# Two adder convolutions, rebuilt from four channels over half an image to one channel over a whole image

## The chip, the cores and the metric

The kernel runs on one core of one Trainium2 chip. The metric is the time of one execution on the device in microseconds (us), the median of three runs. The engines are TensorE (PE in the profile; its weight loads are PEld), VectorE (DVE), ScalarE (ACT), GpSimd (POOL) and SyncE (SP, which here only issues transfers). They run side by side, each works through its own instructions in order, and they meet through semaphores.

## The reference, cut to what matters

A batch of 4 images of 128 channels by 64 by 64 positions goes through four layers: attention over positions, a pair of shift and adder convolutions, a gated attention block, and a selective scan. The change is in the second layer, which does this twice, the second time on the normalised result of the first:

```python
def shift_conv(x, w):            # 3x3 convolution, weights rounded to powers of two
    return conv(x, shift_quant(w), padding=1)

def adder_conv(x, w):            # 3x3, stride 1, pad 1: out = -sum |patch - weight|
    patches = conv_general_dilated_patches(x, (3, 3), padding=1)
    p = patches.reshape(N, Cin * 9, H * W)
    def per_channel(wc):
        return -jnp.sum(jnp.abs(p - wc[None, :, None]), axis=1)
    return lax.map(per_channel, w.reshape(Cout, Cin * 9))

out = relu(batchnorm(adder_conv(shift_conv(x, w_shift1), w_add1)))
out = batchnorm(adder_conv(shift_conv(out, w_shift2), w_add2))
return relu(out + x)
```

For each of 128 output channels, each of 9 taps and each image, 128 input channels by 4096 positions of absolute differences are formed and summed over the input channels. No matrix product gives that, and these two sums take two thirds of the kernel.

## The kernel before, in words

All data are fp32, with the 128 channels on the partitions. `shift_adder` (from L266) is called twice; its tiles carry the prefix a1 in the first call and a2 in the second. It quantises the shift weights (L276, L277 and the function above it), convolves image 0 (L319), and then loops over the images. While image b goes through the adder part, the convolution of image b+1 is drawn from a generator, a matmul at a time, between the adder's own matmuls.

**One term, three ways.** |p - w| is formed by ScalarE as an activation (Abs with the weight as a bias, L392), or, since |p - w| = 2 max(p, w) - p - w, by VectorE as a maximum (L403). The nine taps of a channel are shared out: taps 4, 5, 6 and half of tap 7 (scaled by one half) go to ScalarE, taps 0 to 3 to VectorE, and tap 8 is added by VectorE into the tile that ScalarE made for tap 7 (maximum and add in one instruction, L421, in place). A channel so makes 8 tiles: 4 of ScalarE and 4 of VectorE. The sums of p and of w that the maxima leave over are added apart: w as `wsum`, p by matmuls against ones (L348).

**The sum over channels.** TensorE sums a tile over its 128 partitions by a matmul with a weight of 32 columns, of which one is -1 or -2 and the rest 0 (`gather`, L338). The column lands the sum in one row of 32; four column groups of the array take four matmuls at once. In the kernel before, the four groups stand for four output channels, 32 apart.

**The order.** Work goes by image, by half an image (2048 positions), by jj from 0 to 31, and by q from 0 to 3. One q is what I call a step: four channels (32 g + jj), one ScalarE tile and one VectorE tile of 128 by 2048 for each, one L421, 16 gathers of the VectorE tiles and 16 of the ScalarE tiles. Four steps finish four channels for half an image. A half has 128 steps, and a call of `shift_adder` has 1024. The pools give VectorE's tiles 7 buffers and ScalarE's 8 (L293, L294), each of half an image; the sums of a half sit in four PSUM banks, taken from six. In each half, 20 full-width matmuls put the sum of p into the banks (L348), four with the first step and one with each of the next 16. At the end of a half the banks are evicted (L363), counted into the statistics (L364) and stored (L365).

A scheduler orders each engine's instructions ahead of time from the order in which the program states them, and gives out the buffers of each pool; what an engine waits for is then fixed. `layer1` (L437) makes the batch norm's scale from the statistics and gives the second call a loader that normalises the whole image as it comes in (L460 to L462).

Of the kernel before, what the change touches and what calls it, by code (L numbers as in the profile page):

```python
# [8 lines left out]
F32 = mybir.dt.float32  # L9
# [8 lines left out]
B = 4  # L18
# [7 lines left out]
TAPS = 9  # L26

# [12 lines left out]
def rows(ap):  # L40

    return ap.rearrange("p (r w) -> p r w", w=W)
# [223 lines left out]
def shift_adder(tc, cm, load, w_shift, w_add, stats, y_d, tag):  # L266
# [3 lines left out]
    nc = tc.nc  # L270
    with ExitStack() as ctx:
        cp = ctx.enter_context(tc.tile_pool(name=f"{tag}c", bufs=1))
        wqs = cp.tile([P, TAPS, P], F32, name=f"{tag}wq")
        with tc.tile_pool(name=f"{tag}q", bufs=1) as qp:
            ws = qp.tile([P, TAPS * P], F32, name=f"{tag}ws")
            nc.sync.dma_start(ws, w_shift)  # L276
            quantize(nc, qp, ws, wqs.rearrange("p t o -> p (t o)"), tag)  # L277
# [13 lines left out]
        xin_pool = ctx.enter_context(tc.tile_pool(name=f"{tag}x", bufs=1))  # L291
        pb_pool = ctx.enter_context(tc.tile_pool(name=f"{tag}p", bufs=2))
        dp = ctx.enter_context(tc.tile_pool(name=f"{tag}d", bufs=7))  # L293
        ap = ctx.enter_context(tc.tile_pool(name=f"{tag}a", bufs=8))  # L294
        ep = ctx.enter_context(tc.tile_pool(name=f"{tag}e", bufs=2))
        ps_c = ctx.enter_context(tc.tile_pool(name=f"{tag}pc", bufs=2, space=PSUM))
        ps_a = ctx.enter_context(tc.tile_pool(name=f"{tag}pa", bufs=6, space=PSUM))
# [3 lines left out]
        pw = ps_c.tile([P, 1], F32, tag="cv", name=f"{tag}pw")  # L301
        for i, t in enumerate(sum_taps):
            nc.tensor.matmul(pw, wa[:, t, :], cm.one_col, start=(i == 0), stop=(i == len(sum_taps) - 1))
        wsum = cp.tile([P, 1], F32, name=f"{tag}wsum")
        nc.vector.tensor_copy(wsum, pw)

        def fetch(b):
            t = xin_pool.tile([P, HP, HP], F32, tag="xin", name=f"{tag}xin{b}")
            clear_border(nc, t)
            load(b, t[:, 1 : 1 + H, 1 : 1 + W])  # L310
            return t

        def convolution(b, xin, pb):

            for k in range(NB):
                pc = ps_c.tile([P, BK], F32, tag="cv", name=f"{tag}pc{b}_{k}")
                for t in range(TAPS):
                    y, x = divmod(t, 3)
                    nc.tensor.matmul(  # L319
                        pc,  # L320
                        wqs[:, t, :],
                        xin[:, RB * k + y : RB * (k + 1) + y, x : x + W],
                        start=(t == 0),
                        stop=(t == TAPS - 1),
                    )
                    if t == TAPS - 1:
                        nc.vector.tensor_copy(pb[:, 1 + RB * k : 1 + RB * (k + 1), 1 : 1 + W], rows(pc))
                    yield
# [6 lines left out]
        def gather(pa, s, jj, group):  # L335

            for g, (v, d) in enumerate(group):
                nc.tensor.matmul(  # L338
                    pa[s][32 * g : 32 * g + 32, :],
                    pick[v][:, 31 - jj : 63 - jj],  # L340
                    d[:, bass.ts(s, BK)],
                    start=False, stop=False, skip_group_check=True,
                )

        def sum_of_p(pa, s, pb, half, t):
            y, x = divmod(t, 3)
            r = half * H // 2 + RB * s + y
            nc.tensor.matmul(  # L348
                pa[s], cm.ones, pb[:, r : r + RB, x : x + W],
                start=(t == sum_taps[0]), stop=False, skip_group_check=True,  # L350
            )

        def sums_of_p(pa, pb, half):
            for t in sum_taps[1:]:
                for s in range(4):
                    sum_of_p(pa, s, pb, half, t)
                    yield

        def evacuate(b, half, pa):
            for s in range(4):  # L360
                k = 4 * half + s
                o = ep.tile([P, BK], F32, tag="ev", name=f"{tag}ev{b}_{k}")
                nc.vector.tensor_scalar(o, pa[s], wsum, None, ALU.add)  # L363
                nc.vector.bn_stats(stats[:, NB * b + k, :], o)  # L364
                nc.sync.dma_start(y_d[b, :, bass.ts(k, BK)], o)  # L365

        pb = padded(0)
        for _ in convolution(0, fetch(0), pb):
            pass
        done = None  # L370
        for b in range(B):
            pb_next, steps = None, None
            for half in range(2):

                def view(t):
                    y, x = divmod(t, 3)
                    r0 = half * H // 2 + y
                    return pb[:, r0 : r0 + H // 2, x : x + W]

                pa = None  # L380
                for jj in range(32):
                    if b < B - 1 and half == 0 and jj == 1:
                        pb_next = padded(b + 1)
                        steps = convolution(b + 1, fetch(b + 1), pb_next)
                    for q in range(4):

                        act = [None] * 4
                        for g in [q] + [g for g in range(4) if g != q]:
                            co = 32 * g + jj
                            t = HALF_TAP if g == q else ACT_TAPS[q if q < g else q - 1]  # L390
                            at = ap.tile([P, HL], F32, tag="ab", name=f"{tag}a{b}_{half}_{co}_{t}")
                            nc.scalar.activation(  # L392
                                rows(at), view(t), AF.Abs, bias=wn[t][:, co : co + 1],
                                scale=0.5 if g == q else 1.0,
                            )
                            act[g] = (-2.0 if g == q else -1.0, at)

                        dve = []
                        t = DVE_TAPS[q]
                        for g in range(4):  # L400
                            co = 32 * g + jj
                            dt = dp.tile([P, HL], F32, tag="ad", name=f"{tag}d{b}_{half}_{co}_{t}")
                            nc.vector.tensor_scalar(  # L403
                                rows(dt), view(t), wa[:, t, co : co + 1], None, ALU.max
                            )
                            dve.append((-2.0, dt))
                        if pa is None:
                            if done:
                                evacuate(*done)
                            pa = []  # L410
                            for s in range(4):
                                pa.append(ps_a.tile([P, BK], F32, tag="pa", name=f"{tag}pa{b}_{half}_{s}"))
                                sum_of_p(pa, s, pb, half, sum_taps[0])
                                gather(pa, s, jj, dve)
                            sums = sums_of_p(pa, pb, half)
                        else:
                            for s in range(4):
                                gather(pa, s, jj, dve)
                        co = 32 * q + jj
                        at = rows(act[q][1])  # L420
                        nc.vector.scalar_tensor_tensor(  # L421
                            at, view(MAX_TAP), wa[:, MAX_TAP, co : co + 1], at, ALU.max, ALU.add
                        )
                        for s in range(4):
                            gather(pa, s, jj, act)
                        next(sums, None)
                        if steps and (q == 1 or q == 3 and jj % 4 < 2):
                            next(steps, None)
                done = (b, half, pa)
            if steps:  # L430
                for _ in steps:
                    pass
            pb = pb_next
# [3 lines left out]
def layer1(tc, cm, w_shift1, w_add1, g1, b1, w_shift2, w_add2, g2, b2, x1d, y1d, y2d):  # L437


    nc = tc.nc  # L440

    def batchnorm_scale(stats, gamma, name):
        mv = cm.pool.tile([P, 2], F32, name=f"mv{name}")
        nc.vector.bn_aggr(mv, stats.rearrange("p a s -> p (a s)"))
        sc = cm.pool.tile([P, 1], F32, name=f"sc{name}")
        cm.rstd(nc, sc, mv[:, 1:2])
        nc.vector.tensor_tensor(sc, sc, gamma, ALU.mult)
        return mv[:, 0:1], sc

    vec = {}  # L450
    for name, src in (("g1", g1), ("b1", b1), ("g2", g2), ("b2", b2)):
        vec[name] = cm.pool.tile([P, 1], F32, name=f"bn_{name}")
        nc.sync.dma_start(vec[name], col(src))

    stats1 = cm.pool.tile([P, B * NB, 6], F32, name="stats1")
    shift_adder(tc, cm, lambda b, t: nc.sync.dma_start(t, rows(x1d[b])), w_shift1, w_add1, stats1, y1d, "a1")
# [747 lines left out]
```

## Time and profile before

| what | us |
|---|---|
| median of three runs | 23555.58 (23554.83 to 23556.7) |
| the profiled execution, its own time | 23557.55 |
| its span from first to last instruction | 23555.8 |
| first call's adder part, from ScalarE's first Abs to its last | 2049.9 to 9944.4 |
| second call's adder part | 10030.0 to 17926.5 |

The page gives busy times of an execution: PE 21606.2 us (92% of the span), DVE 20116.0 (85%), ACT 19647.4 (83%), POOL 3766.7 (16%). Those are averages over stages with different limits. In the groups of instructions, each row is a line, engine and operation, with shapes, count, busy time, mean length of one in ns, and the idle time before it. The strip of forty digits cuts the span into slices, each digit a tenth of busy time. In the timeline, each row is a start, a length, and a run of equal instructions with no idle time between them, so that the spacing of n equal instructions is the length less that of one, over n - 1. A matmul of fp32 appears as two records.

### The profile page before, as it was taken

What the parts mean: (1) busy time and instruction counts of PE and PEld (TensorE: products, weight loads), DVE (VectorE), ACT (ScalarE), POOL (GpSimd) and SP (SyncE); (2) the same over time, 40 slices, a digit from 0 to 9 for tenths busy, and PEclk for the clock granted to TensorE, in tenths of its full rate; (3) what the DMA queues carried; (4) which work ended last, traced back from release to release, by engine and by line L of the source; (5) the groups of instructions that cost most, each with busy time, mean ns of one, the idle gap of its engine ahead of it and who ended that gap; (6) DMA issues with size and microseconds to landing.
All of it is one profiled execution on the core that took longest, in us unless ns stands there. A gap on an engine that the chain in (4) does not pass through costs nothing. (4 is left out here: it accounts for less than half of the span.)

```text
span 23555.8 us, 348033 instructions
## 1 busy us (share of the span) xinstructions
PE 21606.2 (92%) x146624; PEld 7799.2 (33%) x146624; DVE 20116.0 (85%) x15018; ACT 19647.4 (83%) x13700; POOL 3766.7 (16%) x1710
## 2 busy tenths in 40 slices
PE   9999999999999999999999999999997567677777
PEld 4443333333333333333333333333332222222222
DVE  7887999999999999889999999999997665777776
ACT  5666999999999999899999999999996336555555
POOL 5662000000000000000000000000000000577776
PEclk9999999999999999999999999999998776899999
DMA  0000000000000000000000000000000002788876
GB/s 14 9 5 12 1 3 7 1 3 5 3 3 1 3 1 3 8 5 3 5 3 1 5 5 1 3 1 3 3 1 32 0 3 96 182 195 194 194 192 163
DMA packets 174504, 809.07 MB, mean 34 GB/s; under 512 B 22716, under 2 KB 23364, under 8 KB 102788
## 3 DMA queue, kind: packets, MB, share of 16 engines
q1 hardware_dynamic: 172356, 778.42, 13.0%
q8 instruction: 1146, 18.78, 0.3%
q10 hardware_dynamic: 576, 8.39, 0.1%
q14 instruction: 426, 3.49, 0.0%
HBM read 658.15 MB, written 128.58 MB: 33 GB/s over the span
## 5 line engine op out<-in xcount | busy, mean ns | idle before, releaser
L392 ACT ACTIVATE a1a<-a1pb,a1wn 128x2048 f32<-128x2048 f32 x4096 | 7793.2, 2001 | 198.3 <-PE a1pa L338 101.3
L392 ACT ACTIVATE a2a<-a2pb,a2wn 128x2048 f32<-128x2048 f32 x4096 | 7791.9, 1999 | 136.2 <-PE a2pa L338 94.0
L403 DVE TENSOR_SCALAR a2d<-a2pb,a2wa 128x2048 f32<-128x2048 f32 x4096 | 4993.4, 1281 | 212.9 <-PE a2pa L338 212.4
L403 DVE TENSOR_SCALAR a1d<-a1pb,a1wa 128x2048 f32<-128x2048 f32 x4096 | 4992.1, 1281 | 207.2 <-PE a1pa L338 206.9
L338 PE MATMUL a2pa<-a2a,a2pick 128*32 128x512 f32 x32768 | 4576.3, 593 | 31.5 <-ACT a2a L392 31.5
L338 PE MATMUL a1pa<-a1a,a1pick 128*32 128x512 f32 x32768 | 4569.2, 593 | 31.5 <-ACT a1a L392 31.5
L338 PE MATMUL a2pa<-a2d,a2pick 128*32 128x512 f32 x32768 | 4436.8, 594 | 46.3 <-DVE a2d L403 46.0
L338 PE MATMUL a1pa<-a1d,a1pick 128*32 128x512 f32 x32768 | 4434.3, 594 | 47.2 <-DVE a1d L403 46.9
L421 DVE SCALAR_TENSOR_TENSOR a1a<-a1pb,a1wa,a1a 128x2048 f32<-128x2048 f32 x1024 | 2406.1, 2350 | 323.6 <-ACT a1a L392 323.6
L421 DVE SCALAR_TENSOR_TENSOR a2a<-a2pb,a2wa,a2a 128x2048 f32<-128x2048 f32 x1024 | 2406.1, 2350 | 314.1 <-ACT a2a L392 314.1
L338 PEld LDWEIGHTS a2pa<-a2a,a2pick 128*32 128x32 f32 x32768 | 1489.1, 110 | 2370.1 <-issue 2061.7
L338 PEld LDWEIGHTS a1pa<-a1a,a1pick 128*32 128x32 f32 x32768 | 1486.9, 110 | 2370.7 <-issue 2045.3
L962 PE MATMUL mg<-h,ident 128*128 128x512 f32 x4096 | 1982.8, 634 | 298.1 <-ACT m L971 227.4
L338 PEld LDWEIGHTS a2pa<-a2d,a2pick 128*32 128x32 f32 x32768 | 1347.1, 109 | 2472.1 <-issue 1935.5
L338 PEld LDWEIGHTS a1pa<-a1d,a1pick 128*32 128x32 f32 x32768 | 1345.4, 109 | 2471.8 <-issue 1913.8
L947 DVE TENSOR_TENSOR_SCAN h<-da,h,dbu 128x1024 f32<-128x1024 f32 x768 | 1804.2, 2349 | 87.0 <-POOL dbu L933 4.7
L962 PEld LDWEIGHTS mg<-h,ident 128*128 128x128 f32 x4096 | 787.1, 201 | 1529.4 <-issue 856.9
L186 POOL TENSOR_TENSOR ssum<-ssum,et 128x512 f32<-128x512 f32 x960 | 1230.3, 1282 | 232.9 <-ACT et L181 166.1
L975 POOL TENSOR_TENSOR m<-m,C 128x2048 f32<-128x2048 f32 x256 | 1157.7, 4522 | 605.2 <-ACT m L971 435.9
L933 POOL TENSOR_TENSOR dbu<-du,B 128x2048 f32<-128x2048 f32 x256 | 1153.6, 4529 | 26.3 <-DMA du<-du_d 26.3
L151 ACT COPY et<-pe 128x512 f32<-128x512 f32 x1024 | 596.6, 583 | 591.6 <-PE pe L149 575.9
L149 PE MATMUL pe<-q,k 128*128 128x512 f32 x2048 | 1051.1, 596 | 8.6 <-DVE mx L159 8.1
(267 smaller groups left out, 13672.1 us busy)
## 6 DMA issues: line engine op xcount, KB each, us to landing
dl<-delta_d SPq DMA_DIRECT2D x256, 1024.0 KB
du<-du_d SPq DMA_DIRECT2D x256, 1024.0 KB
xs_d<-xs SPq DMA_DIRECT2D x8, 2048.0 KB
sz_d<-sz SPq DMA_DIRECT2D x64, 256.0 KB
delta_d<-dv SPq DMA_DIRECT2D x32, 512.0 KB
du_d<-du SPq DMA_DIRECT2D x32, 512.0 KB
y_d<-ye SPq DMA_DIRECT2D x64, 256.0 KB
yx<-xs_d SPq DMA_DIRECT2D x64, 256.0 KB
```

Of the source, the lines that this page charges most:

```text
L149: nc.tensor.matmul(pe, k[:, bass.ts(j, P)], unit[u, "q"], start=True, stop=True)
L151: nc.scalar.copy(et, pe)
L186: nc.gpsimd.tensor_tensor(unit[u, "sum"], unit[u, "sum"], at, ALU.add)
L338: nc.tensor.matmul(pa[s][32 * g : 32 * g + 32, :], pick[v][:, 31 - jj : 63 - jj], d[:, bass.ts(s, BK)], start=False, stop=False, skip_grou ...
L392: nc.scalar.activation(rows(at), view(t), AF.Abs, bias=wn[t][:, co : co + 1], scale=0.5 if g == q else 1.0,)
L403: nc.vector.tensor_scalar(rows(dt), view(t), wa[:, t, co : co + 1], None, ALU.max)
L421: nc.vector.scalar_tensor_tensor(at, view(MAX_TAP), wa[:, MAX_TAP, co : co + 1], at, ALU.max, ALU.add)
L933: nc.gpsimd.tensor_tensor(t, du, by_states(b, h)[0], ALU.mult)
L947: nc.vector.tensor_tensor_scan(t[:, cols][:, s], da[:, s], st[n, "dbu", h][:, cols][:, s], 0.0 if e % 4 == 0 else st["last"], ALU.mult, AL ...
L962: nc.tensor.matmul(pm, cm.ident, st[n, way, h][:, bass.ts(k, BK)], start=(way == 0), stop=(way == 1))
L975: nc.gpsimd.tensor_tensor(m, m, by_states(tiles[n][0], h)[1], ALU.mult)
```

## The change

`shift_adder` is rebuilt around a whole image and one channel at a time:

- A tile is 128 by 4096, a whole image. The four column groups of TensorE take four position blocks of 512 of one channel's tile, and two PSUM banks take the eight blocks. A row of the banks is a channel, and 32 channels fill them.
- Every fourth channel (`extra`) adds tap 3 by a maximum and add in place into the tile of tap 1, so that it has two of those and 7 tiles to gather, and not 8.
- The sums of p are made once an image, in column groups, copied to a tile, and added at the eviction. They are drawn from the same generator as the next image's convolution.
- VectorE's tiles have 3 buffers and ScalarE's 4, of a whole image each.
- The convolution's input comes in 8 blocks of rows (with one row beside on either end) from 3 buffers, and not as an image; the normalising of the second call goes by block too.
- Both quantisations stand ahead of the first call.
- Rows of the statistics no longer stand where the channels do, so they go to DRAM and back ahead of the scale.

```diff
-        dp = ctx.enter_context(tc.tile_pool(name=f"{tag}d", bufs=7))
-        ap = ctx.enter_context(tc.tile_pool(name=f"{tag}a", bufs=8))
+        dp = ctx.enter_context(tc.tile_pool(name=f"{tag}d", bufs=3))
+        ap = ctx.enter_context(tc.tile_pool(name=f"{tag}a", bufs=4))
...
-        xin_pool = ctx.enter_context(tc.tile_pool(name=f"{tag}x", bufs=1))
+        xin_pool = ctx.enter_context(tc.tile_pool(name=f"{tag}x", bufs=3))
...
+        def gather(pa, jj, v, d, first=False):
+
+            for k in range(2):
+                for g in range(4):
+                    nc.tensor.matmul(
+                        pa[k][32 * g : 32 * g + 32, :],
+                        pick[v][:, 31 - jj : 63 - jj],
+                        d[:, bass.ts(4 * k + g, BK)],
+                        start=first, stop=False, skip_group_check=True,
+                    )
...
+        def evacuate(b, c, pa, sp):
+            for k in range(2):
+                o = ep.tile([P, BK], F32, tag="ev", name=f"{tag}ev{b}_{c}_{k}")
+                nc.vector.scalar_tensor_tensor(o, pa[k], wsum[:, c : c + 1], sp[:, k, :], ALU.add, ALU.add)
+                nc.vector.bn_stats(stats[:, c, 2 * b + k, :], o)
+                to = y_d[b, 32 * c : 32 * c + 32, :].rearrange("j (k g w) -> k g j w", k=2, g=4)
+                nc.sync.dma_start(to[k], o)
...
+                ah = absolute(HALF_TAP)
+                d = maximum(DVE_TAPS[0])
+                if late:
+                    gather(*late)
+                gather(pa, jj, -2.0, d, first=(jj == 0))
...
+                d = maximum(DVE_TAPS[1])
+                if extra:
+                    plus_maximum(d, DVE_TAPS[3])
+                else:
+                    gather(pa, jj, -2.0, d)
+                a = absolute(ACT_TAPS[0])
+                if co % 3 < 2:
+                    next(steps, None)
+                gather(pa, jj, -1.0, a)
+                a = absolute(ACT_TAPS[1])
+                if extra:
+                    gather(pa, jj, -2.0, d)
+                    gather(pa, jj, -1.0, a)
+                    plus_maximum(ah, MAX_TAP)
+                    gather(pa, jj, -2.0, ah)
+                    d = maximum(DVE_TAPS[2])
+                    a = absolute(ACT_TAPS[2])
+                    gather(pa, jj, -1.0, a)
+                    late = (pa, jj, -2.0, d)
+                else:
+                    plus_maximum(ah, MAX_TAP)
+                    gather(pa, jj, -2.0, ah)
+                    gather(pa, jj, -1.0, a)
+                    d = maximum(DVE_TAPS[2])
+                    gather(pa, jj, -2.0, d)
+                    a = absolute(ACT_TAPS[2])
+                    d = maximum(DVE_TAPS[3])
+                    gather(pa, jj, -2.0, d)
+                    late = (pa, jj, -1.0, a)
...
+        nc.sync.dma_start(at, stats.rearrange("p c s v -> p c (s v)"))
+        byco = lp.tile([P, 4, 2 * B * 6], F32, name=f"byco{name}")
+        for c in range(4):
+            nc.sync.dma_start(
+                byco[32 * c : 32 * c + 32], at[:, c, :].rearrange("(g j) s -> j g s", g=4)
             )
```

`absolute`, `maximum` and `plus_maximum` are the three instructions of L392, L403 and L421 with tiles of 4096. Names below: h is the tile of tap 7 (with tap 8 added in), a4 to a6 are ScalarE's other tiles, d0 to d3 VectorE's.

## The prediction

> **What bounds the kernel now.** First the strip of the page, to see where the engines are full:
>
> ```profile
> PE   9999999999999999999999999999997567677777
> DVE  7887999999999999889999999999997665777776
> ACT  5666999999999999899999999999996336555555
> PEclk9999999999999999999999999999998776899999
> ```
>
> From digit 5 to 30 three engines stand at nine tenths together. That stage is the two adder parts; the windows (PE, PEld, DVE, ACT and POOL busy) give it exactly:
>
> ```profile
> 2049.90:9944.40 7894.50, 7815.85 (x66276) 2741.18 (x66278) 7351.58 (x5197) 7793.11 (x4096) 5.33 (x10) 1.00 0.01 3
> 10030.00:17926.50 7896.50, 7818.72 (x66276) 2744.18 (x66278) 7357.29 (x5200) 7802.38 (x4099) 5.26 (x10) 1.00 0.01 3
> ```
>
> Which engine binds is seen in the timeline. A stretch without sums of p:
>
> ```profile
> 10499.75 32.35 ACT L392 ACTIVATE a2a<-a2pb,a2wn 128x2048 f32<-128x2048 f32 x17
> ...
> 10501.77 2.35 DVE L421 SCALAR_TENSOR_TENSOR a2a<-a2pb,a2wa,a2a 128x2048 f32<-128x2048 f32 x1 [0.46 <-ACT a2a L392]
> 10504.04 4.87 DVE L403 TENSOR_SCALAR a2d<-a2pb,a2wa 128x2048 f32<-128x2048 f32 x4
> 10509.37 2.35 DVE L421 SCALAR_TENSOR_TENSOR a2a<-a2pb,a2wa,a2a 128x2048 f32<-128x2048 f32 x1 [0.47 <-ACT a2a L392]
> ```
>
> ScalarE never pauses; VectorE waits for it each step. Its spacing is (32.35-2.00)/16 = 1.897 us, a step is 4 x 1.897 = 7.59. A stretch with sums of p:
>
> ```profile
> 8001.02 1.13 PE L348 MATMUL a1pa<-a1pb,ones 128*128 128x512 f32 x2
> 8002.08 3.64 PE L338 MATMUL a1pa<-a1d,a1pick 128*32 128x512 f32 x32
> 8005.54 3.62 PE L338 MATMUL a1pa<-a1a,a1pick 128*32 128x512 f32 x32
> ...
> 8001.17 7.70 ACT L392 ACTIVATE a1a<-a1pb,a1wn 128x2048 f32<-128x2048 f32 x4 [0.41 <-PE a1pa L338]
> 8009.23 7.70 ACT L392 ACTIVATE a1a<-a1pb,a1wn 128x2048 f32<-128x2048 f32 x4 [0.36 <-PE a1pa L338]
> ```
>
> Here TensorE binds: ScalarE waits for it, and the step is 8009.23-8001.17 = 8.06. So 1024 x 7.59 = 7772 of a part's 7894.5; the other 122, or 15 per half, lie where the sums of p are. A round of four gathers takes 0.43 us per record ((3.64-0.593)/7, a record being 593 ns long), so a step's 16 rounds take 6.9.
>
> The changed tiles are twice as long. Other lines of this trace have such instructions:
>
> ```profile
> L779 ACT ACTIVATE xs<-xs,cb 128x4096 f32<-128x4096 f32 x8 | 29.7, 3707 | 24.2 <-DVE xs L776 24.2
> L774 DVE TENSOR_SCALAR xs<-pre,cw 128x4096 f32<-128x4096 f32 x8 | 18.8, 2354 | 49.3 <-ACT pre L772 49.3
> L776 DVE SCALAR_TENSOR_TENSOR xs<-pre,cw,xs 128x4096 f32<-128x4096 f32 x24 | 107.6, 4485 | 0.9
> ```
>
> **What the Trainium skill says.** "ScalarE: Activation LUTs", What ACT_TABLE_LOAD costs: with a pointer bias 280 ns and 0.833 ns an element, and neighbours overlap by 93 ns. The trace agrees: 2001 ns at 2048, 3707 at 4096, overlap 2001-1897 = 104. "VectorE: DVE Perf Modes", the perf-mode tier table: fp32 tensor_scalar in SBUF runs at twice the rate, and a second tensor operand takes that away. So 2354 against 4485 ns: a maximum moved into a max-add costs VectorE nearly double. "TensorEngine Tiling (Array Packing)", Key Properties: column tiles work independently, and a change of mode drains the array. The trace shows both: 0.43 us per round, and L348 costing the step over a microsecond for its 0.86 of streaming. "Perfetto Trace Analysis", Optimization Strategy: the same gap repeating on the engine that should be full can mean too few buffers. Before, no such gap stands outside the sums of p; my forecast is that the change makes one.
>
> **The change, part by part.**
>
> *Loads per four channels of an image* (eight steps before, 8 x 7.59 = 60.7). Spacings at 4096: Abs 3.707-0.10 = 3.61; maximum 2.354-0.08 = 2.27 (overlap: 1.281-(4.87-1.28)/3); max-add 4.485-0.08 = 4.40; a gathered tile 4 rounds x 0.43 = 1.72, ending 0.16 later. ScalarE: 16 x 3.61 = 57.8. VectorE: 15 maxima and 5 max-adds (16 and 4 without the extra) = 34.1+22.0 = 56.1. TensorE: 31 tiles x 1.72 = 53.3, and 82 generator steps over 32 periods, 2.6 x 0.86+0.3 = 2.5, together 55.8. The extra takes 1.72 off an engine that doesn't bind and adds 2.1 to VectorE. By these sums alone ScalarE would give 57.8.
>
> *The wait that the change adds.* The order built for the changed kernel has, in each extra channel, VectorE: d0, max-add into h, d1, d2, max-add into d1. TensorE: d0, a4, generator steps, d1, a5, h, a6, d2. So everything behind d1 on TensorE waits for VectorE's last instruction of the channel; and with 4 buffers the next channel's a4 waits until the old a5 is gathered. Let 0 be the end of the max-add into d1. Gathers of d1 and a5 end at 0.05+1.72+1.72+0.16 = 3.65; a4 of channel 1 starts at 3.7. Eleven spacings on (a4, a5, a6; two channels of h, a4, a5, a6; h of channel 4) h starts at 3.7+39.7 = 43.4 and ends at 47.1. Then VectorE: max-add into h 4.40, d1 2.27, d2 2.27, max-add into d1 4.485: 60.6. That is a ring through three engines; it closes each period, and ScalarE stands idle 60.6-57.8 = 2.8 at its start. TensorE clears its backlog meanwhile (53.3+2.5 < 60.6). The other waits have slack: h of channel 3 needs channel 2's a4 gathered, 18.2 (end of h)+4.40+2.35+1.72+1.88+0.15 = 28.7, and ScalarE comes there at 28.9.
>
> *A part's sum.* 32 periods x 4 images x 60.6 = 7757; the first period of all has no ring yet, -3: 7754. The sums of p become 40 matmuls an image, 10 rounds of four (8.6 us against 17 a half); nearly half go ahead of the first gather, while VectorE makes the first tile, the rest in waits for a max-add. The 122 of before goes to nothing; if the cover failed, 4 x 8.6 = 34 a part come back. The convolution's steps lie in the extra channels' waits too. Eviction has the same count of instructions. Against 7894.5: -140.
>
> *Second part.* Normalising by block: 8 activations of 640 columns an image, about 0.73 us each on ScalarE (0.63 at 512 columns), in the ring: 3 x 8 x 0.73 = 17, bounds 0 and 25. 7771 against 7896.5: -125. The block loads are issued from SP beside the stores; with 3 buffers they lead by two blocks of 7.7 us. Pads add POOL memsets, and POOL is idle there.
>
> *Start.* Before, quantising took 1984.6 to 1995.1, the image's load to 2008.0, and the first Abs came at 2049.9, after five blocks of convolution (7.72 apart). Now: a second quantising in the same buffer (load 4.7, work 10.5, all in front of the convolution's tiles) +15.2; first block instead of image, 4.7 for 12.9, -8.2; eight blocks and a copy ahead of the first Abs, since it reads the whole image, 8 x 7.72+0.8 = 62.6 for 41.8, +20.8. Sum +28, bounds 15 and 38.
>
> *Between the parts* (85.5 before, last Abs to first). Max-add into d1 2.6 after the last Abs, five gathers 8.8, eviction 2.7 (L363 and L364, 1.41 and 1.28 a pair); statistics out and back, two hops of 4.5 each (576 KB took 4.7; bounds 2 and 9); scale 3.1, one block normalised 1.4, convolution 62.6: 90.2, +5 (0 to 14). After the second part (29.8 before, to the residual's first instruction) the same 14.1+9+3.1 = 26 stands against it, but the hops queue with the residual's loads: 0, bounds -4 and +8.
>
> Sum: -140-125+28+5 = -232 from the profiled execution's 23557.6 (span and 1.8 around it): 23325. The median is 2 lower: **23323**.
>
> **Rivals.**
>
> *The hand-off binds as well (no change).* Channel by channel, h, its max-add, d1, two gathers, next h makes 14.2 against ScalarE's 14.4. If semaphores and drains cost 0.7 more per hand-off, each of two channels loses 0.5 and the period is 61.5: 232 is used up, 23550. Against it: VectorE starts 0.03 us after ScalarE in the trace of before.
>
> *The gather slows down (slower).* Before, the four groups of a round stream four tiles; now four blocks of one tile. If the round takes 0.50 instead of 0.43, up to the unoverlapped 0.593, then TensorE needs 31 x 2.0+2.5 = 64.5 and is the bound: 3.9 x 256 = 1000 more, 24330. It decides from 0.474, where TensorE reaches 61.5. Against it: the groups' records show no such sharing before, with the same partitions read.
>
> *The ring doesn't bind (faster still).* ScalarE alone sets the pace if the old a5 is gathered ahead of d1's wait: 57.8, 2.8 x 256 = 717 less, 22610. The order speaks against it, and so it would be the case that the change does what it says, fuller engines, without a new wait.
>
> **How the numbers follow.** Ring 0.80, 23323, its own range 23230 to 23420 (0.3 us a period is 77, and the edges' bounds). No change 0.06, slower 0.07, unbound 0.07. The range goes to 23460 on the dear side, into the hand-off's case. 0.2% is about what a measurement can tell from no change: faster 0.88, same 0.05, slower 0.07.
>
> **What would show it.** Right: Abs of 4096 about 3.61 apart; ScalarE idle about 2.8 us once in 16 Abs, ended by TensorE; VectorE idle ahead of the max-add into h, ended by ScalarE; four channels every 60.6; no stretch with full-width sums; adder parts of 7754 and 7771; the first Abs some 28 later. Wrong: TensorE without pauses, rounds over 0.47, or pauses in every channel.

## The result, and the profile after

| | before | after |
|---|---|---|
| median, us | 23555.2 (23541.1 to 23556.7, four runs) | 23729.7 (23719.8 to 23740.0, four runs) |
| ratio to before | | 1.0075 (95% interval 1.0059 to 1.009) |
| profiled execution, its span | 23555.8 | 23738.2 |

The changed kernel is 0.75% slower. I had forecast 23323 and a range up to 23460. Split by the same marks as in the prediction, the 182 us of span stand so:

| stretch | before | forecast | after | after less forecast |
|---|---|---|---|---|
| to the first Abs | 2049.9 | 2077.9 | 2083.9 | +6 |
| adder part of the first call | 7894.5 | 7754 | 7940.8 | +187 |
| between the parts | 85.5 | 90.2 | 101.1 | +11 |
| adder part of the second call | 7896.5 | 7771 | 7958.9 | +188 |
| from the last Abs to the end | 5629.3 | 5629 | 5653.4 | +24 |

So nearly all of the miss lies in the two adder parts. The strip of the page:

```profile
PE   9998999998998888899999899888886557677777
DVE  7887999998998898889999999989986665777776
ACT  5666999999999999899999999999996335555555
PEclk9999999999999999999999999999997776899999
```

TensorE drops to eight tenths here and there; a strip in tenths says no more. The windows of the two parts (same columns as before) say it:

```profile
2083.95:10024.70 7940.75, 7287.52 (x64156) 2102.17 (x64148) 7257.19 (x2652) 7409.81 (x2048) 8.51 (x34) 0.97 0.01 3
10125.90:18084.80 7958.90, 7288.98 (x64156) 2101.45 (x64148) 7268.17 (x2674) 7425.30 (x2070) 8.27 (x30) 0.97 0.01 3
```

TensorE is busy for 528 us less than before, ScalarE for 383 less, and yet the first part is 46 longer: no engine is full any more. The granted clock of TensorE (the third figure from the end) is 0.97, and was 1.00. The waits (engine and line, who released it, total, times, longest):

```profile
DVE aa L431 <- ACT aa L420: 1051.3, 756, 3.0
...
ACT aa L420 <- PE a1pa L377: 530.6, 127, 5.8
...
PE a1pa L377 <- DVE da L431: 469.5, 125, 5.5
```

This is the forecast ring, in its place: ScalarE waits for TensorE once in each of the 127 later periods of four channels, and TensorE waits for the max-add into d1. Only the size is off: 530.6/127 = 4.2 us and not 2.8. The timeline of TensorE in the last image shows where the rest comes from:

```profile
9638.07 1.90 PE L377 MATMUL a1pa<-aa,a1pick 128*32 128x512 f32 x16
9639.78 1.90 PE L377 MATMUL a1pa<-da,a1pick 128*32 128x512 f32 x16
9641.50 1.90 PE L377 MATMUL a1pa<-aa,a1pick 128*32 128x512 f32 x16
9648.84 3.62 PE L377 MATMUL a1pa<-da,a1pick 128*32 128x512 f32 x16 [5.44 <-DVE da L431]
9652.25 5.36 PE L377 MATMUL a1pa<-aa,a1pick 128*32 128x512 f32 x48
```

A tile's 16 records take 1.90 us. After 5.44 us without work the same 16 take 3.62: TensorE restarts at about half speed. The granted clock says the same. Around another such wait (5.45 us, with d1's tile from 3918.68 on) the windows read, the clock again third from the end:

```profile
3912.00:3914.00 2.00, 1.23 (x12) 0.13 (x4) 2.00 (x1) 2.00 (x2) 0.00 (x0) 1.00 0.00 0
3919.00:3920.00 1.00, 1.00 (x8) 0.20 (x4) 1.00 (x1) 0.61 (x1) 0.00 (x0) 0.50 0.00 0
3922.00:3923.00 1.00, 1.00 (x12) 0.24 (x8) 1.00 (x1) 0.00 (x0) 0.00 (x0) 1.00 0.00 0
```

Earlier in an image the wait is covered:

```profile
2924.05 1.90 PE L377 MATMUL a1pa<-aa,a1pick 128*32 128x512 f32 x16
2925.88 4.56 PE L345 MATMUL a1pc<-a1xin,a1wq 128*128 128x512 f32 x10
2931.39 1.92 PE L377 MATMUL a1pa<-da,a1pick 128*32 128x512 f32 x16 [0.95 <-DVE da L431]
```

The scheduler has pulled the generator's matmuls (the next image's convolution) into the wait, 0.95 us of it is left, and d1's tile takes 1.92. The generator's matmuls last for 23 of 32 periods in image 0, some 16 and 11 in images 1 and 2, and in image 3 they cover none. So the images get longer one by one, from first to last Abs 1954, 1974, 1989 and 2010 us, the last one with the least work. In the first part 48 of 127 periods take 60.7 (two, at the start, 57.9), and 77 take 62.0 to 63.7, 62.9 in the mean.

### The profile page after: what moved, and what is told of

It reads as the page before. It is cut to its first block, busy times and chain, and to the rows that moved or that the text cites. A ratio compares the mean times of both kernels' runs of the same rounds, so it can differ in the third digit from the quotient of the medians.

```text
span 23738.2 us, 322750 instructions
## 1 busy us (share of the span) xinstructions
PE 20618.5 (87%) x142828; PEld 6548.0 (28%) x142828; DVE 19928.9 (84%) x9942; ACT 18891.3 (80%) x9632; POOL 3774.5 (16%) x1774
## 5 line engine op out<-in xcount | busy, mean ns | idle before, releaser
L420 ACT ACTIVATE aa<-a1pb,a1wn 128x4096 f32<-128x4096 f32 x2048 | 7409.8, 3712 | 661.5 <-PE a1pa L377 530.6
L420 ACT ACTIVATE aa<-a2pb,a2wn 128x4096 f32<-128x4096 f32 x2048 | 7411.9, 3711 | 536.6 <-PE a2pa L377 533.3
L427 DVE TENSOR_SCALAR da<-a1pb,a1wa 128x4096 f32<-128x4096 f32 x1920 | 4407.7, 2348 | 152.8 <-PE a1pa L377 152.5
L427 DVE TENSOR_SCALAR da<-a2pb,a2wa 128x4096 f32<-128x4096 f32 x1920 | 4407.5, 2348 | 149.2 <-PE a2pa L377 149.2
L377 PE MATMUL a2pa<-da,a2pick 128*32 128x512 f32 x30720 | 3668.5, 612 | 670.3 <-DVE da L431 470.9
L377 PE MATMUL a1pa<-da,a1pick 128*32 128x512 f32 x30720 | 3668.9, 612 | 653.7 <-DVE da L431 469.5
L377 PE MATMUL a2pa<-aa,a2pick 128*32 128x512 f32 x32768 | 3750.9, 599 | 2.2 <-ACT aa L420 2.1
L377 PE MATMUL a1pa<-aa,a1pick 128*32 128x512 f32 x32768 | 3748.0, 598 | 2.2 <-ACT aa L420 2.0
L431 DVE SCALAR_TENSOR_TENSOR aa<-a2pb,a2wa,aa 128x4096 f32<-128x4096 f32 x512 | 2295.5, 4483 | 529.3 <-ACT aa L420 529.3
L431 DVE SCALAR_TENSOR_TENSOR aa<-a1pb,a1wa,aa 128x4096 f32<-128x4096 f32 x512 | 2295.6, 4483 | 522.1 <-ACT aa L420 522.1
```

What stands on the lines that cost most here:

```text
L377: nc.tensor.matmul(pa[k][32 * g : 32 * g + 32, :], pick[v][:, 31 - jj : 63 - jj], d[:, bass.ts(4 * k + g, BK)], start=first, stop=False, s ...
L420: nc.scalar.activation(rows(at), view(t), AF.Abs, bias=wn[t][:, co : co + 1], scale=0.5 if half else 1.0)
L427: nc.vector.tensor_scalar(rows(dt), view(t), wa[:, t, co : co + 1], None, ALU.max)
L431: nc.vector.scalar_tensor_tensor(rows(at), view(t), wa[:, t, co : co + 1], rows(at), ALU.max, ALU.add)
```

## The experiments

The theory, called the clock theory below: TensorE is slowed by its wait in the ring, and d1's tile, inside the ring, so takes longer. Rivals: the hand-off itself costs that, whatever TensorE did before; the whole-image form costs it; the ring isn't what binds. Every ratio below is to the kernel before.

**Filling the wait, first try.** `fill` streams the padded image against ones into a spare bank, with nothing that reads it:

```diff
                 if extra:
+                    fill(pb)
                     gather(pa, jj, -2.0, d)
```

> Seven rounds of four matmuls that nobody reads (3.0 us at 0.43 a round, into a spare PSUM bank) stand on TensorE ahead of d1's gathers in every extra channel, so that 2.4 of the 5.45 us of waiting are left; nothing else is changed, and no instruction waits for them but TensorE's own next. Clock theory (TensorE is slowed to half speed after some microseconds of idling, and d1's tile then takes 3.0 instead of 1.7): d1's tile takes 1.72 in all periods, granted clock 1.00, four channels every 60.7 throughout, (62.02-60.7) x 128 + (62.17-61.0) x 128 = 320 less: 23410. Rival (the hand-off from VectorE to TensorE or the freshly written tile costs the 1.3, whatever TensorE did before): periods stay at 62 to 63.7, 23730, or more by what the filler adds.

Measured: 23955.4, ratio 1.0167 (1.0150 to 1.0184). Not the time that the clock theory gave (the rival's "or more" would allow it), and the filler was mis-sized: a matmul has two records, so seven rounds are 56 records and take 6.0 us, more than the wait. In images 0 to 2, where the generator's steps found no wait left to lie in, most periods are 62.9 to 64.6. But in image 3, where the filler stands alone, the periods are 61.1 against some 63, the image takes 1957 in place of 2010, and the clock of the run is 0.959 again. That speaks for the clock.

> The same with one round (0.43 us) in place of seven, so that 5.0 us of waiting are left. Clock theory: TensorE still idles too long, d1's tile takes 3.0, periods of 62 to 63.7 stay, 23730. Rival (any matmul between a5's place and d1's does it, for example by the order of the queue): as with seven rounds, 23410.

Measured: 23615.6, ratio 1.0024 (1.0015 to 1.0033), 114 less than the changed kernel, which neither theory gave. In the trace the filler isn't where I put it: nothing held it back, and the scheduler pulled it ahead into other channels. TensorE had 102 waits of about 5.4 us and not 152; all 102 restarts were slow. Fifty slow restarts fewer at some 2.2 us (62.9 less 60.7) are 110 of the 114. So it is a test of how often, not of how long.

**Filling it rightly.** Five rounds, reading the finished a5 so that they stay put, in channels where the generator has run dry:

```diff
                 if extra:
+                    if co >= (92, 68, 48, 20)[b]:
+                        fill(a)
                     gather(pa, jj, -2.0, d)
```

> The changed kernel with five rounds of four unread matmuls (5 x 0.86 = 4.3 us: a matmul has two records, so a round of four takes twice the 0.43 that the seven rounds were sized with) on TensorE between a4 and d1 of an extra channel. They read the finished tile a5, so that they can't be pulled ahead, and stand only in channels where the generator has run dry in the trace of the changed kernel (from channel 92, 68, 48 and 20 of the four images). About 1.2 of the 5.45 us of waiting is left. Clock theory: d1's tile takes 1.72 in these periods too, four channels every 60.7 all through: 170 + 150 = 320 less than the changed kernel, 23410, within 40. Rival (the wait costs the same whatever TensorE does in it): 23730 or more.

Measured: 23409.0, ratio 0.9937 (0.9920 to 0.9953). This is the clock theory's number, and the rival falls. The same place in TensorE's timeline, in this kernel:

```profile
9618.10 1.90 PE L387 MATMUL a1pa<-aa,a1pick 128*32 128x512 f32 x16
9619.82 4.47 PE L316 MATMUL a1fill<-aa,ones 128*32 128x512 f32 x40
9625.46 1.92 PE L387 MATMUL a1pa<-da,a1pick 128*32 128x512 f32 x16 [1.17 <-DVE da L441]
```

4.5 us of useless work ahead of d1's tile take 1.7 off it. 117 of 127 periods now take 60.7, and the parts are 7782 and 7802. Useless work made the changed kernel faster than the one before.

**Cutting the ring.** Three ways: no extra channels; d1 last on TensorE; a fifth buffer.

```diff
-                extra = co % 4 == 3
+                extra = False
```

> No extra channels: all 128 channels of an image are made as the other three of four are, with 8 tiles each and one max-add. Ring theory: nothing on TensorE waits for VectorE's last instruction of a channel, ScalarE's 16 x 3.61 = 57.8 sets the period (VectorE 16 x 2.27 + 4 x 4.40 = 53.9, TensorE 32 x 1.72 + 2.5 = 57.5), TensorE never idles for 3 us: 23730 - 4.2 x 128 - 4.2 x 128 = 22655; if TensorE's 57.5 binds with what hand-offs add, up to 58.8 and 22910. Rival (the whole-image form itself costs the time: four position blocks of one tile, or hand-offs in each channel): 62 and 23700, or worse, since a tile more is gathered.

Measured: 23171.7, ratio 0.9835 (0.9820 to 0.9850). The ring is gone and so is 558 us; the whole-image form isn't what costs. But 22655 isn't reached. In image 3 most periods are 57.8; in images 0 to 2 most are 59.9 to 61.7. There TensorE runs as follows:

```profile
4583.59 1.90 PE L377 MATMUL a1pa<-da,a1pick 128*32 128x512 f32 x16
4585.87 1.92 PE L377 MATMUL a1pa<-da,a1pick 128*32 128x512 f32 x16 [0.39 <-DVE da L427]
4587.73 1.13 PE L345 MATMUL a1pc<-a1xin,a1wq 128*128 128x512 f32 x2
4588.78 5.36 PE L377 MATMUL a1pa<-aa,a1pick 128*32 128x512 f32 x48
```

Eight tiles of 1.72 and waits of 0.4 to 0.5 all but fill a channel's 14.45; a step of the convolution, 1.05, finds no gap, and ScalarE waits 0.97 for it. I read this as the hand-off ring of a channel, the prediction's first rival, just below ScalarE's pace: it shows as soon as the extra channels' gaps are gone. That isn't shown, since no run without extra channels had a fifth buffer; how much is the ring and how much TensorE's own load stays open.

```diff
                 if extra:
-                    gather(pa, jj, -2.0, d)
                     gather(pa, jj, -1.0, a)
                     plus_maximum(ah, MAX_TAP)
                     gather(pa, jj, -2.0, ah)
+                    d1 = d
                     d = maximum(DVE_TAPS[2])
+                    gather(pa, jj, -2.0, d)
                     a = absolute(ACT_TAPS[2])
                     gather(pa, jj, -1.0, a)
-                    late = (pa, jj, -2.0, d)
+                    late = (pa, jj, -2.0, d1)
```

> The extra channels stay, but on TensorE the gathers of a5, h, d2 and a6 go ahead of d1's, which is gathered last in its channel; the order of VectorE and ScalarE is as in the changed kernel. Ring theory: old a5 no longer waits for the max-add into d1, so the ring of three engines is cut and TensorE has no long wait: 57.8 a period, 22655. If the extra max-add is what costs (VectorE's 56.1 with waits), 59 to 60.6: 22960 to 23370. Rival (the ring is not what binds): no change, 23730.

Measured: 22960.9, ratio 0.9745 (0.9731 to 0.9760). By its number this is the middle case of the expectation, whose reason, VectorE's load, the next runs don't bear out. A period takes 59.2; ScalarE still waits 1.5 us in 106 of 127 periods:

```profile
ACT aa L420 <- PE a1pa L377: 162.1, 106, 3.4
```

Around an extra channel VectorE works without a pause for over 24 us, TensorE waits up to 2.9 us for its next tile, and some of those waits end in a slow restart as well.

> The kernel with d1 gathered last, and an extra channel in every eighth place in place of every fourth. If the extra channel's load on VectorE is what costs its 1.4 us a period, half of it goes: 22960 - 0.7 x 256 = 22780. If TensorE binds instead (31.5 x 1.72 and the generator's steps, 57.3, with hand-offs as in the kernel without extras): 59.2, 23000 to 23060.

Measured: 23039.9, ratio 0.9779 (0.9765 to 0.9794): TensorE's case. Fewer extra channels make it dearer. The difference lies in images 0 to 2 (59.6 to 59.7 a period in the first part, against 59.1 to 59.4); image 3, with no convolution beside it, takes 58.6 against 58.7. So the seven-tile channels are the gaps into which the convolution goes.

```diff
-        ap = ctx.enter_context(tc.tile_pool(name=f"{tag}a", bufs=4))
+        ap = ctx.enter_context(tc.tile_pool(name=f"{tag}a", bufs=5))
```

> The changed kernel with 5 buffers for ScalarE's tiles in place of 4, nothing else. Ring theory: the next channel's a4 no longer waits until the old a5 is gathered, only the tile after it does, which is 3.6 us later: four channels every 62.1 - 3.6 = 58.5, 23730 - 3.6 x 256 = 22810, with TensorE still waiting some 5 us for the max-add into d1 and still slowed after it. Rival (TensorE's wait and slow start bind by themselves, the buffer doesn't matter): 62, 23730.

Measured: 22767.6, ratio 0.9665 (0.9650 to 0.9679), 42 from the forecast. One buffer is worth 962 us to the changed kernel. TensorE's waits for the max-add into d1 are still there, 256 us of them in the first part, up to 4.2; ScalarE sees little of them:

```profile
PE a1pa L377 <- DVE da L431: 255.7, 127, 4.2
...
ACT aa L420 <- PE a1pa L377: 58.9, 50, 2.8
```

> The kernel with d1 gathered last (22961) and 5 buffers for ScalarE's tiles. There ScalarE still loses 1.4 us a period to a4 waiting for old tiles while TensorE waits for VectorE after an extra channel. If that is the shallow pool: 57.8 to 58.2 a period, 22960 - 1.2 x 256 = 22650, to 22720. Rival (VectorE, busy without a pause after an extra channel, is what binds there): 59, 22900 to 22960.

Measured: 22669.9, ratio 0.9623 (0.9608 to 0.9637), as forecast. With the same load on VectorE, periods are now 57.9 and 58.1 in the mean, and ScalarE never waits long:

```profile
ACT aa L420 <- PE a2pa L377: 14.8, 23, 1.7
ACT aa L420 <- PE a1pa L377: 12.2, 20, 2.0
```

7413.8 us of the first part against 128 x 57.8 = 7398: this is ScalarE's floor.

**The edges.** Both with d1 last and 5 buffers. The first moves the matmuls of `wsum` after `convolution(0, ...)`, the second also moves the second `quantized` behind the first `batchnorm_scale`.

> The kernel with d1 last and 5 buffers (22670), with the 160 one-column matmuls of the sums of w after image 0's convolution in each call, and not ahead of it. My reading of the changed kernel's start is that they take 5.86 us of TensorE on the path, between the load of the weights and the convolution. If so: first Abs 5.9 earlier (2077.0), and between the parts 0 to 6 less, as far as the scale waited for them; the 5.9 of TensorE come back at the first gathers, where TensorE has 2 us a period to spare, at no cost or up to 4 a call. 22655 to 22666. Rival (the load of the first block ends the wait, the matmuls lie beside it): first Abs unchanged, 22670 or up to 8 more.

Measured: 22654.7, ratio 0.9616 (0.9603 to 0.9629), against 0.9623 without it: the intervals overlap. In the traces the first Abs is 4.2 earlier (2078.7 against 2082.9) and the stretch between the parts 5.7 shorter (88.7 against 94.4), so the reading holds by its place. (The expectation calls them 160 matmuls; they are 80, with two records each.)

> The same, and the second quantising after the first call's statistics instead of ahead of the first call. My price for it at the start was 15.2 us: first Abs at 2062. Between the parts it has the round trip of the statistics (16 us from their store to the scale) beside it, and costs 0 if it fits there, up to 15 if its load queues behind them. 22640 if it fits, 22655 if not. Rival (it was hidden at the start by the load of the image): first Abs unchanged, 22660 or more.

Measured: 22640.1, ratio 0.9612 (0.9599 to 0.9626). The first Abs is 14.3 earlier, at 2064.4, but the stretch between the parts is 13.2 longer: the quantising doesn't fit beside the statistics. By these two it nets 1 us. In the profiled executions all but 1 of the 31 us between them lie behind the adder parts, where the code is the same and the executions profiled here spread from 5625 to 5656; what moved it is open. That the median is the 22640 forecast for the case that it fits is luck: the trace shows that it doesn't fit.

## Why the prediction was wrong, by its steps

*Loads:* right. Abs start 3.61 apart, the other kinds last as taken, a tile takes 1.72 where TensorE is warm (at full clock), and ScalarE reaches 57.8 where nothing holds it. The second part is 18 longer than the first, where the normalising was put at 17.

*The ring:* right in mechanism, place and warm size (60.72 where TensorE stays warm, forecast 60.6). **The step that failed is "Gathers of d1 and a5 end at 0.05+1.72+1.72+0.16 = 3.65."** I took d1's tile from steady stretches, where TensorE never rests, and put it where the same ring has just made TensorE wait 5.4 us. In the slow periods d1's tile takes 3.0 to 3.4: in the lines above 9652.25-9648.84 = 3.41, and in the period before, the three tiles behind it are slowed too and take 6.15 in place of 5.15. The step as a whole, from the end of the max-add into d1 to the start of the a4 that waits:

```profile
9644.30 4.48 DVE L431 SCALAR_TENSOR_TENSOR da<-a1pb,a1wa,da 128x4096 f32<-128x4096 f32 x1
9654.31 57.87 ACT L420 ACTIVATE aa<-a1pb,a1wn 128x4096 f32<-128x4096 f32 x16 [4.55 <-PE a1pa L377]
```

That is 9654.31-9648.78 = 5.5 where I put 3.7. Over the first part it is 3.8 in 48 of 127 rings, and 5.1 to 6.8, 6.0 in the mean, in the other 79. The sum: 77 slow periods x (62.9-60.7) = 169, and 128 x (60.72-60.6) = 15 for the warm size, against +187 found in the first part. (The written terms of the ring add up to 60.5 and not 60.6; that is 0.1 of the warm size.) By experiment: right-sized filler took 158 and 157 off the parts.

The page of the Trainium skill to look at was there. "TensorE: Matmul & The Clock Gate", in Part 1, says that TensorE falls to half of its clock after an idle window of about 3.4 us and needs about as long of work to come back. This trace agrees on the half clock (0.50 after the wait) and about on the way back (1.00 some 3 us later); on how long the pause has to be, it differs, as the last section shows. I cited other pages and never asked how long TensorE would stand idle in the ring.

*Sums of p:* right; no stretch of full-width sums is left. But with them went TensorE's even load. That the generator's steps lie in the waits was no mere cover either: as long as they last, they keep the clock up.

*Start, +6:* the 80 one-column matmuls of `wsum` (L317, two records each), 5 before, stand alone on TensorE ahead of the convolution:

```profile
2012.88 5.86 PE L317 MATMUL a1pw<-one_col,a1wa 128*32 128x1 f32 x160 [38.46 <-DMA a1wa<-in_w_add]
2018.67 64.47 PE L345 MATMUL a1pc<-a1xin,a1wq 128*128 128x512 f32 x144
```

I had left them out; moving them gave 4.2 back. They account for most of the 3.7 by which the convolution starts later than my sum had it (2015.0). The other 2.7 are the convolution itself, 65.3 to the first Abs for 62.6. It too starts at half clock (0.50 in the windows from 2018.7 to 2022), and so it did before: the 41.8 of five blocks hold this, and 8 x 7.72 left it out.

*Between the parts, +11:* the hops. SP's issues there:

```profile
10040.14 0.51 SPq L492 DMA_DIRECT2D stats_d<-stats  x1
10040.75 0.52 SPq L290 DMA_DIRECT2D a2wa<-in_w_add  x1
10048.36 1.75 SPq L495 DMA_DIRECT2D byco<-stats_d  x4
```

The way out takes 8.2, and L499 starts at 10056.1, 7.7 later: 15.9 where I put 9. That wait is partly `wsum`'s (5.7 came back when it was moved). The restarted convolution takes 65.0 to the first Abs for 62.6, another 2, and the last gathers about 1.

*End, +24:* 14.5 are there at the residual's first instruction, the same hops and slow gathers with the residual's loads between; the other 10 arise in unchanged code and are within its spread.

*Rivals:* the slow gather fell, since the round is 0.43 as before wherever TensorE is warm; only behind the pause is it 0.85. The kernel came out slower all the same, by a way that I had not listed. The hand-off, if it is that, binds only once the ring is cut. Unbound, 22610, is what d1 last with the fifth buffer comes near (22670).

## What to carry to other kernels

When a change puts a wait on TensorE, price the wait's length before the work behind it. After the pauses of 5.4 us here TensorE ran at half clock for some 3 to 6 us (each slow ring lost 1.3 to 3.0), and where that work lies inside the ring, every turn pays. Outside it the same restarts cost little: with the fifth buffer TensorE still waited and restarted slowly, and ScalarE hardly saw it. A ring through three engines is cut at its cheapest place, here by one more buffer or one gather moved behind others, and both together come within 0.3% of the bound that the loads alone give (22670 against 22610). Filler against a cold clock has to be tied to the place by its operand and sized to less than the wait.

## What the runs showed of the hardware

I had not expected how short a pause is enough. In eleven traces (the changed kernel and the ten experiments) I counted the pauses of over 0.3 us ahead of a gathered tile, with TensorE at full clock before (idle from the end of one record to the start of the next). A restart is called slow where the tile's 16 records take over 2.1 us in place of 1.9:

| idle, us | restarts | slow |
|---|---|---|
| 0.3 to 1.5 | 5190 | 0 |
| 1.5 to 2.5 | 506 | 136 |
| 2.5 to 3.5 | 198 | 120 |
| over 3.5 | 426 | 425 |

The shortest pause with a slow restart is 1.89 us, the longest without one 3.54. The granted clock in the same traces shows why no single length decides. Apart from the first in each trace, every change of it lies on a grid of 3.41 us, whose phase differs from run to run and stays within a run. I took the windows of this grid at full clock, from the first Abs of the first part to the last of the second, by the share of the window in which TensorE was busy:

| TensorE busy | windows | half clock in the next |
|---|---|---|
| under 39% | 584 | 584 |
| 39 to 47% | 206 | 105 |
| over 47% | 47794 | 1 |

So 1.9 us can be enough inside one window, and 3.5 us shared by two windows need not be. (The ends of matmuls are modelled in the profile, so the shares are rough.) The Trainium skill, "TensorE: Matmul & The Clock Gate", Part 1, has a free-running window of about 3.4 us, and the grid agrees with it; but the page asks for an idle window, and here one was enough in which TensorE was busy for up to two fifths of the time.
